# Two attention visits of a product stream merged into one, with PSUM banks shared and sums of 512 columns

## The chip, the cores and the metric

The kernel runs on one core of a Trainium2 chip. The metric is the device time of one execution in microseconds (us), lower being better. Engines are named as in the profile: PE is TensorE (PEld its weight loads), DVE is VectorE, ACT is ScalarE, POOL is GpSimd, SP is SyncE, which issues most DMAs.

## The reference

All data are fp32. x is 8 x 1024 x 1024, the memory is 8 x 64 x 512, W_mem is 1024 x 512, W_gate is 1024 x 2048.

```python
memory_proj = einsum('bme,de->bmd', memory, W_mem)
scores = einsum('bnd,bmd->bnm', x, memory_proj) / sqrt(1024)
attn = softmax(scores)
memory_context = einsum('bnm,bmd->bnd', attn, memory_proj)
gate = sigmoid(einsum('bnf,df->bnd', concat([x, memory_context]), W_gate) + b_gate)
fused = x + gate * memory_context
out = fused * rsqrt(mean(fused**2) + 1e-6) * norm_w
```

## The kernel before

**Setup.** The memory is projected, and the right half of W_gate is applied to it once, so that the gate's second half becomes attention times a 64-row table. Each batch has a tile `mg` of 128 partitions: rows 0 to 63 hold the projection, rows 64 to 127 the projection times the gate weights, with the bias. One set of attention weights `attnT` thus gives both the context (from the upper half) and the gate's addend (from the lower half); `attnT` holds the attention on both halves of its partitions.

**The main loop** takes 16 quads, each of 512 rows of x (four row tiles of 128; two quads are a batch). The gate's product of x with the left half of W_gate is done by two levels of the Winograd form of Strassen's method. The outer level has seven products, in the fixed order of `ORDER`: 1, 6, 7, 5, 4, 2, 3. Each outer product is an inner Winograd product of seven steps, A, B, C, D, A again, E, F; a step is two calls of `mm` (L92), which the profile shows as four matmul passes of 256 columns, since fp32 takes two passes. Steps count slots, 7 to an outer product and 49 to a quad.

**Left operands.** POOL forms four sums `l` for each inner product, one product ahead (`inner_s`): s1 and s2 in the first slots (part 0), s3 and s4 in slot 5 (part 1, slot 2 ahead of product 5). s1 goes into D, s2 into B, s3 into C, s4 into F. DVE forms the outer sums `s` of 1024 columns (`outer_s`), and transposes the next quad's x in eight parts of 512 columns (`transpose_x`, L355): two beside product 5, one in slot 36, two beside product 2, one in slot 38, and two in slots 42 and 43.

**Inner sums.** ACT copies A's sum to p1 (L821). DVE forms u2 = p1 + B, u3 = u2 + C, u4 = u2 + D. POOL adds u3 twice and u4 once, 256 columns at a time, into the output blocks (`pre`, the pre-sums: gate<-gate,u), and DVE adds the sums A, D, E and F from PSUM into the same blocks (`fin`). Product 5 has two blocks to add to, product 1 none to start from. All of an engine's instructions keep the order in which the program issues them.

**A visit** is what the change is about. In each of products 5, 4, 2 and 3, after the second A, PE does eight pairs of passes with the 64-row operands: the context `pc` from the upper half of the rows and the gate's addend from the lower half, which is accumulated onto A, F, E and D. The two halves of the rows run side by side. For its addends product 5 and 2 use attention itself, or the difference of two row tiles' attention (`attn_difference`, one instruction of DVE). After a visit come the sigmoid of the gate block (ACT, L668), `gated` (DVE: gate times pc, gate<-gate,pc), and, later in the next quad, `residual` (a DMA of POOL's queue that adds x), `square` (ACT), and `norm` (DVE, L697: two of 512 columns for each row tile), and the store.

**Order.** `at(slot, fn)` puts a function ahead of the product step of that slot; `step()` runs what is due. `mid((q, o), fn)` puts a function after the visit of product o (`beside`). The scores of the next quad (psT, 16 calls) come after the visit of product 3, their transposes (sc) after product 6's B, the attention's transposes (pa) after product 7's D.

**PSUM.** Five banks b0 to b4 turn over among the products' sums, sc holds the scores and the transposes, and two banks (ctx) hold the two pc.

Of the kernel before, what the change touches and what calls it, by code (L numbers as in the profile page):

```python
# [8 lines left out]
F32 = mybir.dt.float32  # L9
AF = mybir.ActivationFunctionType  # L10
ALU = mybir.AluOpType
# [9 lines left out]
def tile_gated_cross_attention_rmsnorm(  # L21
# [72 lines left out]
    def tt(eng, o, a, b, op):  # L94
        pin(eng.tensor_tensor(o, a, b, op))  # L95
# [4 lines left out]
    def t4k(pool, shape, tag, name):  # L100
        return pool.tile(shape, F32, tag=tag, name=name)
# [9 lines left out]
    banks = [f"b{i}" for i in range(5)]  # L111

    def bank(n, shape, name):
        return ps.tile(shape, F32, tag=banks[n % 5], name=name)

# [3 lines left out]
    pz = bank(0, [P, C], "pz")  # L119
# [89 lines left out]
    pt = [bank(4, [P, BM], "pt0")]  # L209
    pt += [ps_ctx.tile([P, BM], F32, tag="ctx", name=f"pt{k}") for k in (1, 2)]  # L210
    pt += [ps.tile([P, BM], F32, tag="sc", name="pt3")]
# [20 lines left out]
    setup_banks = ["b0", "b1", "b2", "b3", "b4", "ctx", "ctx", "sc"]  # L232
# [169 lines left out]
    def scores(q):  # L402

        pst = ps.tile([P, 2 * P], F32, tag="sc", name=f"psT{q}")
# [10 lines left out]
        sTs[q] = t4k(small, [P, 2, P], "sT", f"sT{q}")  # L415
        pin(nc.scalar.copy(sTs[q].rearrange("p t c -> p (t c)"), pst))

    def transpose_scores(q):
        sc = ps.tile([P, 4, M], F32, tag="sc", name=f"sc{q}")
# [24 lines left out]
    def transpose_attn(q):  # L444
        attn = attns.pop(q)
        pa = ps.tile([P, 2, P], F32, tag="sc", name=f"pa{q}")
# [9 lines left out]
        at = attnTs[q] = t4k(small, [P, 6, P], "attnT", f"attnT{q}")  # L456
# [146 lines left out]
    def at(slot, fn, *args):  # L603
        due.setdefault(slot, []).append(lambda: fn(*args))
# [5 lines left out]
    ORDER = ((1, None), (6, None), (7, None), (5, (1, 1, 2)), (4, (1, 0, 2)), (2, (0, 0, 0)), (3, (0, 1, 4)))  # L610
    SLOTS = 49

    def plan(q):
        t0 = SLOTS * q
        nxt = q + 1 < NQ
        order = [o for o, _ in ORDER]
        for i, o in enumerate(order):
            for part, t in ((0, 1), (1, 2 if o == 7 else 5)):
                if i + 1 < len(order):
                    at(t0 + 7 * i + t, inner_s, q, order[i + 1], part)  # L620
                elif nxt:
                    at(t0 + 7 * i + t, inner_s, q + 1, order[0], part)
# [141 lines left out]
    def outer_product(q, o, ext):  # L764

        nonlocal slot, banks
        l11, l12, l21, l22 = quarters(left(q, o))
        s1, s2, s3, s4 = (L2[q, o][:, i, :, :] for i in range(4))
        kb = {}

        def product(name, tag, lhsT, s, start=True):
            nonlocal slot
            step()
            if name not in kb:
                kb[name] = ps.tile([P, C], F32, tag=banks[tag], name=f"k{name}{q}_{o}")
            for k in range(2):
                mm(kb[name], lhsT[:, k, :], w_op(o, s)[:, k, :], start and k == 0, k == 1)
            slot += 1

        def o_blocks(row, h):  # L780

            for t in (2 * row, 2 * row + 1):
                if (q, t) not in O:
                    O[q, t] = t4k(gpool, [P, D], "gate", f"gate{q}_{t}")
            return [
                O[q, 2 * row + r][:, h * H + n * C : h * H + (n + 1) * C]
                for r in range(2)
                for n in range(2)
            ]


        sums = {
            1: [(o_blocks(0, 0), None)],
            6: [(o_blocks(0, 1), (0, 0))],
            7: [(o_blocks(1, 0), (0, 1))] if o == 7 else [],
            5: [(o_blocks(1, 1), (1, 0)), (o_blocks(0, 1), (0, 1))] if o == 5 else [],
            4: [(o_blocks(1, 0), (1, 0))] if o == 4 else [],
            2: [(o_blocks(0, 0), (0, 0))] if o == 2 else [],
            3: [(o_blocks(0, 1), (0, 1))] if o == 3 else [],
        }[o]  # L800
        sums = [(dst, src and o_blocks(*src)) for dst, src in sums]

        def pre(n, u):

            for dst, src in sums:
                if src is not None:
                    tt(nc.gpsimd, dst[n], src[n], u, ALU.add)

        def fin(n, name, u):
            for dst, src in sums:  # L810
                if src is not None:
                    tt(nc.vector, dst[n], (src if u is None else dst)[n], kb[name], ALU.add)
                elif u is not None:
                    tt(nc.vector, dst[n], u, kb[name], ALU.add)
                else:
                    pin(nc.scalar.copy(dst[n], kb[name]))
# [3 lines left out]
        product("A", 0, l11, R11)  # L820
        pin(nc.scalar.copy(p1, kb["A"]))  # L821
        product("B", 1, s2, T2)
        tt(nc.vector, u2, p1, kb["B"], ALU.add)
        product("C", 2, s3, R12)
        tt(nc.vector, u3, u2, kb["C"], ALU.add)
        pre(3, u3)
        pre(2, u3)
        product("D", 3, s1, T1)
        tt(nc.vector, u4, u2, kb["D"], ALU.add)
        pre(1, u4)  # L830
        product("A", 0, l12, R21, False)
        pcs = []
        if ext:
            row, h, g = ext
            at_, mg = attnTs[q], mgs[q // QPB]
            for n in ("E", "F"):
                kb[n] = ps.tile([P, C], F32, tag=banks[4 if n == "E" else 1], name=f"k{n}{q}_{o}")
            for r, names in ((0, ("A", "F")), (1, ("E", "D"))):
                pc = ps_ctx.tile([P, H], F32, tag="ctx", name=f"pc{q}_{o}_{r}")
                for n in range(2):  # L840
                    cols = slice(h * H + n * C, h * H + (n + 1) * C)
                    mm(
                        pc[:, n * C : (n + 1) * C],
                        at_[0:M, 2 * row + r, :],
                        mg[0:M, cols],
                        n == 0,
                        True,
                    )
                    mm(
                        kb[names[n]],  # L850
                        at_[M:P, g + r, :],
                        mg[M:P, cols],
                        names[n] in "EF",
                        True,
                    )
                pcs.append(pc)
        for fn in beside.pop((q, o), ()):
            fn()
        fin(0, "A", None)
        fin(3, "D", u3)  # L860
        product("E", 4, l22, T4, not ext)
        fin(2, "E", u3)
        if ext:
            sigmoid(q, 2 * row + 1, h)
            last = q + 1 == NQ
            if last:
                at(slot + 2, last_gated, 2 * row + 1, h, pcs[1])
            else:
                at(slot + 1, gated, q, 2 * row + 1, h, pcs[1])
        product("F", 1, s4, R22, not ext)  # L870
        fin(1, "F", u4)
        if ext:
            sigmoid(q, 2 * row, h)
            if last:
                at(slot + 3, last_gated, 2 * row, h, pcs[0])
            else:
                at(slot + 2, gated, q, 2 * row, h, pcs[0])
        if o in (4, 3) and q + 1 == NQ:
            c, d = 2 * ext[0], 2 * ext[0] + 1
# [7 lines left out]
        elif o in (4, 3):  # L887

            row = ext[0]
# [14 lines left out]
        banks = [banks[i] for i in (2, 3, 0, 4, 1)]  # L904
        del L2[q, o]

    for q in range(NQ):
        plan(q)
        for o, ext in ORDER:
            outer_product(q, o, ext)  # L910
# [29 lines left out]
```

## Time and profile before

| what | value |
|---|---|
| median of 3 runs | 971.56 us (971.49 to 972.56) |
| span of the profiled execution | 969.8 us |
| median less that span | 1.8 us |
| PE busy | 957.6 us, 4984 matmul passes |
| DVE busy | 819.9 us, 1484 instructions |
| POOL busy | 763.5 us, 890 instructions |
| ACT busy | 330.4 us, 604 instructions |
| a quad, from psT to the next psT (463.16 and 518.01 us) | 54.85 us |

The page gives the span of the profiled execution, from its first to its last instruction, and no separate time for what lies around it. In a timeline the columns are the start in us, the length in us, the engine, the line, the operation, what is written from what is read, the shapes, and a count where equal instructions were merged; the length of matmuls contains their pipelined end, so the step from start to start is the rate. An idle time ahead of an instruction stands in brackets with what ended it.

### The profile page before, as it was taken

What the parts mean: (1) busy time and instruction counts of PE and PEld (TensorE: products, weight loads), DVE (VectorE), ACT (ScalarE), POOL (GpSimd) and SP (SyncE); (2) the same over time, 40 slices, a digit from 0 to 9 for tenths busy, and PEclk for the clock granted to TensorE, in tenths of its full rate; (3) what the DMA queues carried; (4) which work ended last, traced back from release to release, by engine and by line L of the source; (5) the groups of instructions that cost most, each with busy time, mean ns of one, the idle gap of its engine ahead of it and who ended that gap; (6) DMA issues with size and microseconds to landing.
All of it is one profiled execution on the core that took longest, in us unless ns stands there. A gap on an engine that the chain in (4) does not pass through costs nothing.

```text
span 969.8 us, 14401 instructions
## 1 busy us (share of the span) xinstructions
PE 957.6 (99%) x4984; PEld 772.7 (80%) x4984; DVE 819.9 (85%) x1484; ACT 330.4 (34%) x604; POOL 763.5 (79%) x890
## 2 busy tenths in 40 slices
PE   9999999999999999999999999999999999999995
PEld 8546888788888888788888878788888878888884
DVE  6989879889797988879797978979797978979787
ACT  3000234161423334161433324152433325152345
POOL 4998868778786978878786978878687978878692
PEclk9999999999999999999999999999999999999998
DMA  9857483473919374482918375481917365391712
GB/s 374 273 144 172 88 139 91 118 165 77 173 66 172 111 130 99 111 173 69 182 66 162 101 136 114 102 182 57 193 66 150 112 133 118 88 195 50 189 66 87
DMA packets 70919, 128.32 MB, mean 132 GB/s; under 512 B 12352, under 2 KB 49216, under 8 KB 70592
## 3 DMA queue, kind: packets, MB, share of 16 engines
q1 hardware_dynamic: 61664, 93.86, 37.0%
q0 software_dynamic: 9184, 33.56, 18.8%
q8 instruction: 39, 0.64, 0.3%
q14 instruction: 32, 0.26, 0.1%
HBM read 87.56 MB, written 41.68 MB: 133 GB/s over the span
## 4 chain that ended last, share of the span: by engine, by line
PE 98%; DMA 1%; DVE 0%; ACT 0%; POOL 0%; SPq 0%; issue 0%; DVEq 0%
PE kA L92 20%; PE pc L92 12%; PE kE L92 11%; PE kD L92 10%; PE kF L92 10%; PE kB L92 10%; PE kC L92 10%; PE psT L92 6%; PE pg L92 5%; PE pm L92 2%; DMA wm<-in_w_mem_t 1%; PE pa L449 0%; PE sc L423 0%; DVE gate L755 0%; DVE gate L95 0%; ACT L762 0%
## 5 line engine op out<-in xcount | busy, mean ns | idle before, releaser
L95 POOL TENSOR_TENSOR gate<-gate,u 128x256 f32<-128x256 f32 x336 | 287.8, 888 | 106.9 <-DVE u L95 106.9
L668 ACT ACTIVATE gate<-gate 128x512 f32<-128x512 f32 x128 | 80.6, 631 | 306.3 <-DVE gate L95 305.7
L355 DVE STREAM_TRANSPOSE a<-xq 128x512 f32<-128x512 f32 x128 | 138.2, 1102 | 2.6 <-POOL it L95 2.6
L95 POOL TENSOR_TENSOR l<-a 128x256 f32<-128x256 f32 x128 | 121.7, 951 | 21.7 <-PE kA L92 21.7
L92 PE MATMUL pc<-mg,attnT 64*128 64x256 f32 x512 | 127.5, 389 | 0.0
L92 PE MATMUL kB<-it,l 128*128 128x256 f32 x448 | 115.1, 379 | 0.6 <-DVE gate L95 0.6
L92 PE MATMUL kD<-it,l 128*128 128x256 f32 x448 | 115.0, 379 | 0.0
L92 PEld LDWEIGHTS pc<-mg,attnT 64*128 64x128 f32 x512 | 90.6, 186 | 29.9 <-issue 21.2
L697 DVE SCALAR_TENSOR_TENSOR gate<-gate,ss,nw_sb 128x512 f32<-128x512 f32 x120 | 109.9, 926 | 1.1
L95 POOL TENSOR_TENSOR l<-s 128x256 f32<-128x256 f32 x96 | 79.2, 825 | 34.2 <-PE kF L92 34.1
L92 PE MATMUL kA<-w,a 128*128 128x256 f32 x384 | 98.6, 379 | 0.0
L92 PEld LDWEIGHTS kB<-it,l 128*128 128x128 f32 x448 | 85.0, 190 | 12.5 <-DVE gate L95 1.0
L92 PEld LDWEIGHTS kD<-it,l 128*128 128x128 f32 x448 | 85.1, 190 | 11.6
L95 DVE TENSOR_TENSOR gate<-gate,pc 128x512 f32<-128x512 f32 x128 | 87.0, 680 | 0.4 <-ACT gate L668 0.4
L95 DVE TENSOR_TENSOR gate<-gate,kE 128x256 f32<-128x256 f32 x112 | 45.6, 420 | 47.4 <-PE kE L92 41.4
L92 PEld LDWEIGHTS kA<-w,a 128*128 128x128 f32 x384 | 71.7, 190 | 9.5 <-issue 0.5
L821 ACT COPY u<-kA 128x256 f32<-128x256 f32 x112 | 40.6, 362 | 110.6 <-PE kA L92 106.3
L92 PE MATMUL kE<-it,a 128*128 128x256 f32 x256 | 69.0, 392 | 0.0
L682 ACT ACTIVATE junk<-gate 128x1024 f32<-128x1024 f32 x60 | 63.5, 1058 | 11.2 <-DMA gate<-in_x 10.2
L92 PE MATMUL kA<-t,s 128*128 128x256 f32 x256 | 65.8, 379 | 0.0
L92 PE MATMUL kF<-w,l 128*128 128x256 f32 x256 | 65.7, 379 | 0.0
L92 PE MATMUL kC<-w,l 128*128 128x256 f32 x256 | 65.7, 379 | 0.0
(143 smaller groups left out, 2042.6 us busy)
## 6 DMA issues: line engine op xcount, KB each, us to landing
xq<-in_x SPq DMA_DIRECT2D x64, 512.0 KB, 10.2
gate<-in_x POOLq DMA_DIRECT2D x60, 512.0 KB, 8.3
out<-gate SPq DMA_DIRECT2D x60, 512.0 KB, 2.6
w<-in_w_gate_t SPq DMA_DIRECT2D x8, 512.0 KB, 10.2
w<-in_w_gate_t SPq DMA_DIRECT2D x2, 2048.0 KB, 16.8
mg<-mgd SPq DMA_DIRECT2D x16, 256.0 KB, 3.8
wm<-in_w_mem_t SPq DMA_DIRECT2D x4, 512.0 KB, 6.4
mpd<-mpT SPq DMA_DIRECT2D x4, 512.0 KB, 7.1
```

Source lines behind the costliest of these rows:

```text
L92: pin(nc.tensor.matmul(o, lhsT, rhs, start=start, stop=stop, skip_group_check=True))
L95: pin(eng.tensor_tensor(o, a, b, op))
L355: nc.vector.transpose(A[key][:, :, r * P : (r + 1) * P], chunks(xq[q][:, 4 * t : 4 * t + 4, :], KD)[:, half * KH : (half + 1) * KH],)
L668: pin(nc.scalar.activation(g, g, AF.Sigmoid))
L682: nc.scalar.activation(junk, O[q, t], AF.Square, accum_out=ss[:, t % 2 : t % 2 + 1])
L697: nc.vector.scalar_tensor_tensor(g[:, cols], g[:, cols], rstd[:, t % 2 : t % 2 + 1], nw_sb[:, cols], ALU.mult, ALU.mult,)
L821: pin(nc.scalar.copy(p1, kb["A"]))
```

## The change

- The visits of 5 and 4 are done together, and those of 2 and 3: both after C of the second product (4 or 3), by `visit`. The first product's sums stay in PSUM until then (`held`).
- A product has two banks, `af` for A and F and `ed` for E and D, and there are two such pairs in turn. One bank b takes every B (kB) and one bank c every C (kC); b also takes psT. The visit of the first product puts its two pc into b and c, that of the second into ctx. In product 3 ACT copies the first of these pc to a tile `pe` in SBUF. sc and pa move to ctx.
- The order of steps becomes A, B, C, (visits), E, D, F, A. What was `mid` beside the visit of 5 or 2 comes after that product's C. In the second products D already contains an addend when u4 is taken from it, so F's addend uses a further difference (`NEG`), for which `attn_difference` gets a second instruction.
- The sums in PSUM are added by DVE in 512 columns (`fin_ed`, `fin_af`), POOL's pre-sum with u3 has 512 columns, that with u4 256. For product 1 a copy from PSUM goes from ACT to DVE, in two parts of 256 for row tile 0.
- For the first product of a pair the sums and the sigmoids run after the visits.

```diff
-    ORDER = ((1, None), (6, None), (7, None), (5, (1, 1, 2)), (4, (1, 0, 2)), (2, (0, 0, 0)), (3, (0, 1, 4)))
+    ORDER = (1, 6, 7, 5, 4, 2, 3)
...
+        tt(nc.vector, at[M:P, 6:8, :], at[M:P, 2:6:2, :], at[M:P, 3:6:2, :], ALU.subtract)
...
+    EXT = {5: (1, 1, 2), 4: (1, 0, 2), 2: (0, 0, 0), 3: (0, 1, 4)}
+    SECOND = {4: 5, 3: 2}
+    NEG = {4: 6, 3: 7}
...
+    def visit(q, o, pcs, af, ed):
+
+        row, h, g = EXT[o]
+        at_, mg = attnTs[q], mgs[q // QPB]
+        second = o in SECOND
+        for r, k in ((0, af), (1, ed)):
+            for n in range(2):
+                cols = slice(h * H + n * C, h * H + (n + 1) * C)
+                mm(
+                    pcs[r][:, n * C : (n + 1) * C],
+                    at_[0:M, 2 * row + r, :],
+                    mg[0:M, cols],
+                    n == 0,
+                    True,
+                )
+                left = NEG[o] if second and r == 0 and n == 1 else g + r
+                mm(k[:, n], at_[M:P, left, :], mg[M:P, cols], second and r == 1 and n == 0, True)
+
+    def pre(q, o, u3, u4):
+
+        for dst, src in SUMS[o]:
+            if src is None:
+                continue
+            if u3 is not None:
+                d, a = blocks(q, dst[0], 1, dst[1]), blocks(q, src[0], 1, src[1])
+                tt(nc.gpsimd, d, a, u3.unsqueeze(1).to_broadcast([P, 2, C]), ALU.add)
+            if u4 is not None:
+                d, a = blocks(q, dst[0], 0, dst[1]), blocks(q, src[0], 0, src[1])
+                tt(nc.gpsimd, d[:, 1], a[:, 1], u4, ALU.add)
...
+        step()
+        kc = bank("c", [P, C], f"kC{q}_{o}")
+        product(kc, s3, R12, True)
+        tt(nc.vector, u3, u2, kc, ALU.add)
+        pre(q, o, u3, None)
+        if second:
+            f = SECOND[o]
+            faf, fed, fu3, fu4 = held.pop((q, f))
+            frow, fh, _ = EXT[f]
+            fp = [bank(t, [P, H], f"pc{q}_{f}_{r}") for r, t in enumerate("bc")]
+            visit(q, f, fp, faf, fed)
+            if o == 3 and nxt:
+                pe = t4k(small, [P, H], "pe", f"pe{q}")
+                pin(nc.scalar.copy(pe, fp[0]))
+                fp[0] = pe
+            pcs = [ps_ctx.tile([P, H], F32, tag="ctx", name=f"pc{q}_{o}_{r}") for r in range(2)]
+            visit(q, o, pcs, af, ed)
+        if second:
+            one = slice(0, 1)
+            fin_af(q, f, faf, fu4, one)
+            gate(q, 2 * frow, fh, fp[0], 0)
+            fin_ed(q, f, fed, fu3, one)
+            gate(q, 2 * frow + 1, fh, fp[1], 1)
+            rest = slice(1, 2)
+            fin_af(q, f, faf, fu4, rest)
+            fin_ed(q, f, fed, fu3, rest)
         for fn in beside.pop((q, o), ()):
             fn()
...
+        step()
+        product(ed[:, 0], l22, T4, not second)
+        step()
+        product(ed[:, 1], s1, T1, False)
+        tt(nc.vector, u4, u2, ed[:, 1], ALU.add)
+        pre(q, o, None, u4)
+        first = o in SECOND.values()
+        if first:
+            held[q, o] = af, ed, u3, u4
+        else:
+            fin_ed(q, o, ed, u3)
+        if second:
+            row, h, _ = EXT[o]
+            gate(q, 2 * row + 1, h, pcs[1], 1)
+        step()
+        product(af[:, 1], s4, R22, False)
+        step()
+        product(af[:, 0], l12, R21, False)
+        if not first:
+            fin_af(q, o, af, u4)
+        if second:
+            gate(q, 2 * row, h, pcs[0], 1)
```

`gate` issues the sigmoid and puts `gated` w slots later. `fin_ed` and `fin_af` add a bank of two blocks into the output blocks in one instruction of 512 columns (row tile 0 of product 1, and of 7, takes two of 256).

More of the change, by code (lines that the diff above doesn't have):

```diff
@@ L109, in chunks, with bank @@
         return t.rearrange("p s e -> p (s e)").rearrange("p (m j) -> p j m", j=n)
-    banks = [f"b{i}" for i in range(5)]
-    def bank(n, shape, name):
-        return ps.tile(shape, F32, tag=banks[n % 5], name=name)
+    def bank(tag, shape, name):
+        return ps.tile(shape, F32, tag=tag, name=name)
     zeros = t4k(small, [P, C], "junk", "zeros")
     pin(nc.vector.memset(zeros, 0.0))
-    pz = bank(0, [P, C], "pz")
+    pz = bank("af0", [P, C], "pz")
     for _ in range(4):
@@ L207, in transpose_mem @@
             )
-    pt = [bank(4, [P, BM], "pt0")]
+    pt = [bank("b", [P, BM], "pt0")]
     pt += [ps_ctx.tile([P, BM], F32, tag="ctx", name=f"pt{k}") for k in (1, 2)]
-    pt += [ps.tile([P, BM], F32, tag="sc", name="pt3")]
+    pt += [bank("c", [P, BM], "pt3")]
     def outer_sum(o, a, b, k=slice(0, 4)):
@@ L231, in tile_gated_cross_attention_rmsnorm @@
     (m11, m12), (m21, m22) = mpT
-    setup_banks = ["b0", "b1", "b2", "b3", "b4", "ctx", "ctx", "sc"]
+    setup_banks = ["af0", "ed0", "af1", "ed1", "b", "ctx", "ctx", "c"]
     setup_next = 0
@@ L402, in scores @@
     def scores(q):
-        pst = ps.tile([P, 2 * P], F32, tag="sc", name=f"psT{q}")
+        pst = bank("b", [P, 2 * P], f"psT{q}")
         mpb = mps[q // QPB]
@@ L414, in scores @@
                 )
-        sTs[q] = t4k(small, [P, 2, P], "sT", f"sT{q}")
+        sTs[q] = t4k(small, [P, 2, P], "e", f"sT{q}")
         pin(nc.scalar.copy(sTs[q].rearrange("p t c -> p (t c)"), pst))
     def transpose_scores(q):
-        sc = ps.tile([P, 4, M], F32, tag="sc", name=f"sc{q}")
+        sc = ps_ctx.tile([P, 4, M], F32, tag="ctx", name=f"sc{q}")
         sT = sTs.pop(q)
@@ L445, in transpose_attn @@
         attn = attns.pop(q)
-        pa = ps.tile([P, 2, P], F32, tag="sc", name=f"pa{q}")
+        pa = ps_ctx.tile([P, 2, P], F32, tag="ctx", name=f"pa{q}")
         for t in range(2):
@@ L454, in transpose_attn @@
             )
-        at = attnTs[q] = t4k(small, [P, 6, P], "attnT", f"attnT{q}")
+        at = attnTs[q] = t4k(small, [P, 8, P], "attnT", f"attnT{q}")
         for g in (1, 0):
@@ L615, in plan @@
         nxt = q + 1 < NQ
-        order = [o for o, _ in ORDER]
-        for i, o in enumerate(order):
+        for i, o in enumerate(ORDER):
             for part, t in ((0, 1), (1, 2 if o == 7 else 5)):
-                if i + 1 < len(order):
-                    at(t0 + 7 * i + t, inner_s, q, order[i + 1], part)
+                if i + 1 < len(ORDER):
+                    at(t0 + 7 * i + t, inner_s, q, ORDER[i + 1], part)
                 elif nxt:
-                    at(t0 + 7 * i + t, inner_s, q + 1, order[0], part)
+                    at(t0 + 7 * i + t, inner_s, q + 1, ORDER[0], part)
         if q == 0:
@@ L762, in sqrt_table, with blocks @@
         pin(nc.scalar.activation(t, eps_sb, AF.Sqrt))
-    def outer_product(q, o, ext):
-        nonlocal slot, banks
+    def blocks(q, row, r, h):
+        t = 2 * row + r
+        if (q, t) not in O:
+            O[q, t] = t4k(gpool, [P, D], "gate", f"gate{q}_{t}")
+        return O[q, t].rearrange("p (n c) -> p n c", c=C)[:, 2 * h : 2 * h + 2]
+    SUMS = {
+        1: [((0, 0), None)],
+        6: [((0, 1), (0, 0))],
+        7: [((1, 0), (0, 1))],
+        5: [((1, 1), (1, 0)), ((0, 1), (0, 1))],
+        4: [((1, 0), (1, 0))],
+        2: [((0, 0), (0, 0))],
+        3: [((0, 1), (0, 1))],
+    }
@@ new lines, in tile_gated_cross_attention_rmsnorm @@
+    EXT = {5: (1, 1, 2), 4: (1, 0, 2), 2: (0, 0, 0), 3: (0, 1, 4)}
+    SECOND = {4: 5, 3: 2}
+    NEG = {4: 6, 3: 7}
+    sets = 0
+    held = {}
+    def visit(q, o, pcs, af, ed):
[14 more added lines that the diff above has]
+                mm(k[:, n], at_[M:P, left, :], mg[M:P, cols], second and r == 1 and n == 0, True)
@@ new lines, in pre, with fin_ed @@
+    def pre(q, o, u3, u4):
[8 more added lines that the diff above has]
+                tt(nc.gpsimd, d[:, 1], a[:, 1], u4, ALU.add)
+    def fin_ed(q, o, ed, u3, n=None):
+        for dst, src in SUMS[o][n] if n is not None else SUMS[o]:
+            d = blocks(q, dst[0], 1, dst[1])
+            tt(nc.vector, d, u3.unsqueeze(1).to_broadcast([P, 2, C]) if src is None else d, ed, ALU.add)
@@ new lines, in fin_af @@
+    def fin_af(q, o, af, u4, n=None):
+        for dst, src in SUMS[o][n] if n is not None else SUMS[o]:
+            d = blocks(q, dst[0], 0, dst[1])
+            if src is None:
+                pin(nc.vector.tensor_copy(d[:, 0], af[:, 0]))
+                tt(nc.vector, d[:, 1], u4, af[:, 1], ALU.add)
+            elif src == dst:
+                tt(nc.vector, d, d, af, ALU.add)
+            elif src[0] == dst[0]:
+                a = O[q, 2 * dst[0]].rearrange("p (n c) -> p n c", c=C)[:, 0:4:3]
+                tt(nc.vector, d, a, af, ALU.add)
+            else:
+                tt(nc.vector, d[:, 0], blocks(q, src[0], 0, src[1])[:, 0], af[:, 0], ALU.add)
+                tt(nc.vector, d[:, 1], d[:, 1], af[:, 1], ALU.add)
@@ L767, in outer_product, with gate, product @@
+    def gate(q, t, h, pc, w):
+        sigmoid(q, t, h)
+        if q + 1 == NQ:
+            at(slot + w, last_gated, t, h, pc)
+        else:
+            at(slot + w, gated, q, t, h, pc)
+    def outer_product(q, o):
+        nonlocal slot, sets
         l11, l12, l21, l22 = quarters(left(q, o))
         s1, s2, s3, s4 = (L2[q, o][:, i, :, :] for i in range(4))
-        kb = {}
-        def product(name, tag, lhsT, s, start=True):
+        nxt = q + 1 < NQ
+        af = bank(f"af{sets}", [P, 2, C], f"af{q}_{o}")
+        ed = bank(f"ed{sets}", [P, 2, C], f"ed{q}_{o}")
+        sets ^= 1
+        second = o in SECOND
+        def product(out, lhsT, s, start):
@@ L772, in product @@
             nonlocal slot
-            step()
-            if name not in kb:
-                kb[name] = ps.tile([P, C], F32, tag=banks[tag], name=f"k{name}{q}_{o}")
             for k in range(2):
-                mm(kb[name], lhsT[:, k, :], w_op(o, s)[:, k, :], start and k == 0, k == 1)
+                mm(out, lhsT[:, k, :], w_op(o, s)[:, k, :], start and k == 0, k == 1)
             slot += 1
[L780 to L789, printed above, removed]
@@ L792, in outer_product @@
[L792 to L801, printed above, removed]
@@ L803, in pre @@
[L803 to L816, printed above, removed]
@@ L818, in outer_product @@
         ut = t4k(rot, [P, 4, C], "u", f"u{q}_{o}")
         p1, u2, u3, u4 = (ut[:, i, :] for i in range(4))
[L820 to L856, printed above, removed]
+        step()
@@ new lines, in outer_product @@
+        product(af[:, 0], l11, R11, True)
+        pin(nc.scalar.copy(p1, af[:, 0]))
+        step()
+        kb = bank("b", [P, C], f"kB{q}_{o}")
+        product(kb, s2, T2, True)
+        tt(nc.vector, u2, p1, kb, ALU.add)
+        step()
[15 more added lines that the diff above has]
+            visit(q, o, pcs, af, ed)
@@ L857, in outer_product @@
+        if second:
[7 more added lines that the diff above has]
+            fin_ed(q, f, fed, fu3, rest)
         for fn in beside.pop((q, o), ()):
             fn()
[L859 to L877, printed above, removed]
@@ L878, in outer_product @@
-        if o in (4, 3) and q + 1 == NQ:
-            c, d = 2 * ext[0], 2 * ext[0] + 1
+        step()
[7 more added lines that the diff above has]
+            held[q, o] = af, ed, u3, u4
+        else:
+            fin_ed(q, o, ed, u3)
+        if second:
+            row, h, _ = EXT[o]
+            gate(q, 2 * row + 1, h, pcs[1], 1)
@@ L880, in outer_product @@
+        step()
+        product(af[:, 1], s4, R22, False)
+        step()
+        product(af[:, 0], l12, R21, False)
[3 more added lines that the diff above has]
+            gate(q, 2 * row, h, pcs[0], 1)
+        if second and not nxt:
+            c, d = 2 * row, 2 * row + 1
             if o == 3:
@@ L886, in outer_product @@
                 at(slot + w_, last_norm, t, h_)
-        elif o in (4, 3):
-            row = ext[0]
+        elif second:
             c, d = 2 * row, 2 * row + 1
@@ L903, in outer_product @@
                     at(slot + w_, norm, q, t, h_)
-        banks = [banks[i] for i in (2, 3, 0, 4, 1)]
         del L2[q, o]
@@ L908, in tile_gated_cross_attention_rmsnorm @@
         plan(q)
-        for o, ext in ORDER:
-            outer_product(q, o, ext)
+        for o in ORDER:
+            outer_product(q, o)
     while due:
```

## The prediction

> **What bounds the kernel now.** I read the page from the top: the busy shares, then the chain that ended last.
>
> ```profile
> PE 957.6 (99%) x4984; PEld 772.7 (80%) x4984; DVE 819.9 (85%) x1484; ACT 330.4 (34%) x604; POOL 763.5 (79%) x890
> ...
> PE 98%; DMA 1%; DVE 0%; ACT 0%; POOL 0%; SPq 0%; issue 0%; DVEq 0%
> ```
>
> TensorE (PE) sets the time, and VectorE (DVE) and GpSimd (POOL) are not far behind. Who waited for whom on PE, next, gives 2.1 us in all, one wait of it in the main loop. So time is gained only by shortening PE's own stream, and lost wherever a changed order makes PE wait. Two quads one after another (463.20 to 572.90 us, table by stretches) give 54.85 us of PE in each, with DVE 46.5 and POOL 43.7 us busy: a quad has 8 to 11 us of room there on average. What counts is the order inside it, so I read each engine's timeline in the quad whose product 1 begins at 468.59 us.
>
> PE around the visit of product 4 (passes left out):
>
> ```profile
> 498.79 1.03 PE L92 MATMUL kA<-t,a 128*128 128x256 f32 x4
> 499.74 0.48 PE L92 MATMUL pc<-mg,attnT 64*128 64x256 f32 x1
> ...
> 500.06 0.38 PE L92 MATMUL pc<-mg,attnT 64*128 64x256 f32 x1
> ...
> 500.28 0.38 PE L92 MATMUL pc<-mg,attnT 64*128 64x256 f32 x1
> ...
> 501.67 1.13 PE L92 MATMUL kE<-it,a 128*128 128x256 f32 x4
> 502.64 0.59 PE L92 MATMUL kF<-t,l 128*128 128x256 f32 x2
> ```
>
> Passes follow each other every 0.216 us, a product of four every 0.863 us. At a change of tiling two steps are longer: 499.74 to 500.06 is 0.32, and kE to kF is 0.97. One change costs about 0.197 us (0.31 + 0.32 - 2 x 0.216), a visit has two, so a visit costs 8 x 0.216 + 0.39 = 2.12 us.
>
> POOL, and the PE product that reads its result s3 (`l`):
>
> ```profile
> 491.96 4.17 POOL L95 TENSOR_TENSOR gate<-gate,u 128x256 f32<-128x256 f32 x6 [1.13 <-DVE u L95]
> 496.10 0.72 POOL L95 TENSOR_TENSOR l<-a 128x256 f32<-128x256 f32 x1
> ```
>
> ```profile
> 497.06 1.03 PE L92 MATMUL kC<-t,l 128*128 128x256 f32 x4
> ```
>
> The s3 of product 4 lands at 496.82, and its product C starts at 497.06: 0.24 us of room, with no wait shown. This is the tightest place in the quad.
>
> DVE, just ahead of that:
>
> ```profile
> 489.73 0.51 DVE L95 TENSOR_TENSOR attnT<-attnT 64x256 f32<-64x256 f32 x1
> 490.27 0.42 DVE L95 TENSOR_TENSOR u<-u,kB 128x256 f32<-128x256 f32 x1
> ...
> 490.80 0.75 DVE L697 SCALAR_TENSOR_TENSOR gate<-gate,ss,nw_sb 128x512 f32<-128x512 f32 x1
> 491.47 0.41 DVE L95 TENSOR_TENSOR u<-u,kC 128x256 f32<-128x256 f32 x1
> ...
> 492.13 2.11 DVE L355 STREAM_TRANSPOSE a<-xq 128x512 f32<-128x512 f32 x2
> ```
>
> C of product 5 ended at 489.75 and DVE can read 0.27 us later (kF's product ends at 503.50, its sum starts at 503.77), yet u3 comes only at 491.47: DVE runs 1.4 us late here, and POOL waits for it.
>
> **What the change takes from PE.** The number of matmuls stays. Four visits become two of double length, and four changes of tiling go: 4 x 0.197 = 0.79 us a quad, 12.6 us over 16. A double visit is not in this trace; between nothing saved and all saved I take all, since the second half only continues the same tiling. The new waits of PE on its own earlier writes (pc's second bank in 4, banks of 2) are for work long done: 0.
>
> **Edits that cost nothing.** 512-column sums replace pairs: DVE 0.60 apiece start to start (pc's row, mean 680) against 2 x 0.33. Product 1's copy moves from ACT to DVE (0.35) where DVE has 3.5 us of work in 6.04. ACT's new 512-column copy `pe` has most of the 2.7 us of visits to run in, ACT being 34% busy; without that cover psT would wait its 0.6 us. One bank for kB and one for kC: between two uses lie five products, 4.3 us, except that the visit of 5 or 2 takes both banks right after C, and so waits for u2 and u3. u3 ends 0.27 + 0.41 after C when DVE is on time, and its bank is needed only after half a visit (1.0 us): hidden.
>
> **First cost: product 4's C waits for POOL.** In 5 the visit goes, so C of 4 is due 2.12 us earlier, at 494.94. What feeds it comes later. POOL's queue now reads: pre-sums of 5 with u3 (two of 512), with u4 (two of 256), then s3. No pre-sum of this shape is in the trace: 512-column POOL rows run from 1.27 us (it from w) to 2.27 (w from w, beside DVE); I take 1.27, since the 256-column ones here also run at their undisturbed step of 0.69. Walk:
> - Product 6's u4 stands behind a norm (478.96, 0.98) and ends at 480.35, so POOL's sum with u4 ends at 481.17, where before it ended at 480.89. Its next six operations took 5.28 us: 486.45. Pre-sum of 7: 487.72.
> - DVE waits for it with the 512 sum: 487.85 to 488.45; s sum 1.32, 489.8; two sums of 7, 490.45; attention differences, now two of 0.54, 491.5; u2 491.85; reciprocal and norm 492.7; u3 493.1. That is 1.2 us later than before.
> - POOL: two of 1.27 to 495.75. u4 now stands behind the two transposes (to 495.1), ends at 495.5 and holds nothing up. Two of 0.69: 497.13. A norm runs beside it; the two norms from 499.64 us (2.25 us) lie beside three POOL sums that took 2.99 us instead of 2.07, so 0.46 more for each norm, which I half count: 497.4. s3: 498.1, and 0.05 to PE.
>
> Wait: 498.15 - 494.94 = 3.2 us. Lower bound: s3 lands when it did before, 496.82, 1.9 us. Upper bound: contention in full and 0.3 on the pre-sums, 3.8. Quad 0 has DVE weight sums and quad 15 no transposes there; POOL is what binds, so all 16 count: 51 us.
>
> **Second cost: product 3's C waits for DVE.** Times from the end of 4's C. Half a visit 1.0, then 0.27. DVE's queue: two sums 1.3 to 1.9 and 2.2 to 2.8 (the second after the whole visit of 5), two more 4.0, two norms 5.4, two products with pc 6.6, u4 7.0, sum 7.6, sigmoid on ACT 0.75 (504.11 less 503.37), pc 8.95, sum 9.55, transpose 10.6, pc 11.2, u2 and u3 of product 2 11.85, three transposes 14.95, u4 15.3. POOL: 0.1 + 0.7 for its pre-sum, 0.7 for s3, 0.05: 16.85. PE: two visits 3.85, four products 3.45, product 2 (its visit gone) 6.04, A and B 1.73: 15.07. Wait 1.8 us; before, s3 of 3 landed at 509.92 for a C at 513.40. Bounds 0.9 (0.1 less at each of nine handovers) and 2.7 (both norms beside POOL). Quad 15 has no transposes left: 15 x 1.8 = 27 us. What was queued behind, u2 of product 3, ends at 17.65, as C ends: no third wait. Product 3 with its psT (13.4 us of PE) and product 1 let DVE and POOL catch up.
>
> **Sum.** The profiled span is 969.8 us, 1.8 below the median of the three runs, 971.56; what lies around it I leave alone, and the tail (10.2 us after the last product) loses or gains under 0.5. 971.5 - 12.6 + 51 + 27 = 1037 us.
>
> **A rule that speaks against it.** The array does start slowly in this trace:
>
> ```profile
> 1.19 3.78 PE L92 MATMUL pz<-zeros 128*128 128x256 f32 x8 [1.19 <-DVE zeros L118]
> ```
>
> Eight passes take 3.78 us, about twice the later step of 0.216, while the granted clock reads 1.00. The Trainium skill, TensorE: Matmul & The Clock Gate, section "What's actually happening", says that the array falls to half rate after an idle window of some 3.4 us and needs as long to recover; no row here shows that in mid-run. An estimate from that page: if every first wait set it off, 1.7 us a quad, 27 us more, 1064 us.
>
> **Rivals.**
> - Faster: DVE and POOL keep up, only the 0.79 us counts: 959 us. It decides below 0.79 us of waits a quad. For it: both engines have 8 us of room a quad. Against: s3 of 4 has 0.24 us of room and its product moves 2.12 us forward; even with u3 on time POOL is free only at 490.83, and 3.9 us of pre-sums and 0.7 of s3 end at 495.4, 0.5 late. 6%.
> - Only one wait appears: C of 4 alone 971.5 - 12.6 + 51 = 1010; C of 3 alone 986. For it: the second hangs on the sum of twenty DVE steps. 22%.
> - The array also slows after the waits, or they are at their upper bounds: 971.5 - 12.6 + 61 + 40 = 1060. 14%.
> - The waits just pay for the saving, within 0.2% (about 2 us, what a measurement of this kernel can tell from no change): 2%.
>
> My case has 56%. The lower bounds with the lower rivals reach 1000 (-12.6 + 30 + 13 = 1002), the upper 1062; that leaves out the faster case and part of C of 3 alone. Slower: 56 + 22 + 14 = 92%.
>
> **What would show it.** Right: PE's waits name POOL l before kC in product 4, 2 to 4 us in each quad, and again in product 3; the quad is near 59 us; double visits last 3.85 us; POOL's 512 sums about 1.3 us. Wrong: a quad near 54.1 us and no PE waits, or waits at the visits' banks (DVE u) instead.

## The result, and the profile after

| | before | changed |
|---|---|---|
| median | 971.5 us (970.98 to 972.56) | 1074.2 us (1071.68 to 1076.25) |
| ratio | 1 | 1.1055 (95% interval 1.1038 to 1.1073) |
| span of the profiled execution, its own time | 969.8 us | 1071.8 us, 1073.56 us |
| a quad, psT to psT | 54.85 us | 61.29 us (502.76 to 564.05) |

The change makes the kernel 10.6% slower; 1037 us was forecast, with a range that ended at 1062. The page of the changed kernel, first the busy times, then the engines of the chain that ended last:

```profile
PE 978.6 (91%) x4984; PEld 791.7 (74%) x4984; DVE 829.0 (77%) x1292; ACT 338.2 (32%) x603; POOL 709.2 (66%) x778
...
PE 49%; DVE 30%; POOL 12%; issue 6%; ACT 2%; DMA 1%; DVEq 0%; SPq 0%; POOLq 0%
```

PE no longer carries the chain: 42% of it runs through DVE and POOL. PE is also *busy* for longer (978.6 us against 957.6) with the same 4984 passes, although four changes of tiling a quad are gone. So there are two losses, waiting and slower work. Who waited on PE, next (total us, times, longest):

```profile
PE kC L92 <- POOL l L95: 79.6, 33, 3.6
```

That is all of the main loop's waiting, and 32 of the 33 waits stand where the forecast put them (the other is at C of product 2 in the last quad). PE's timeline in one quad, with the products' passes around C of 4 and C of 3 (in brackets the wait ahead of the line):

```profile
535.40 1.03 PE L92 MATMUL kB<-it,l 128*128 128x256 f32 x4
539.95 1.50 PE L92 MATMUL kC<-t,l 128*128 128x256 f32 x4 [3.52 <-POOL l L95]
...
546.30 1.13 PE L92 MATMUL ed<-it,a 128*128 128x256 f32 x4
...
556.77 1.03 PE L92 MATMUL kB<-it,l 128*128 128x256 f32 x4
559.34 1.13 PE L92 MATMUL kC<-w,l 128*128 128x256 f32 x4 [1.54 <-POOL l L95]
```

PE idles 3.68 us ahead of C of 4 (from the end of B's four passes at 536.27) and 1.71 us ahead of C of 3. Product 4's C and its double visit then take 6.35 us (539.95 to 546.30); the same work in product 3 takes 4.71 (559.34 to 564.05). Why, the table by stretches shows (the stretch, its length, the busy time of PE, PEld, DVE, ACT and POOL, the granted clock as the third number from the end, DMA share and GB/s):

```profile
536.00:540.00 4.00, 0.47 (x3) 0.07 (x2) 2.28 (x4) 1.31 (x2) 4.00 (x6) 1.00 0.30 121
540.00:542.00 2.00, 2.00 (x8) 1.22 (x10) 0.42 (x1) 0.00 (x0) 1.92 (x3) 0.64 0.05 21
542.00:544.00 2.00, 2.00 (x12) 1.65 (x10) 0.42 (x1) 0.00 (x0) 1.29 (x2) 0.50 0.00 0
544.00:546.00 2.00, 2.00 (x22) 1.74 (x20) 1.55 (x4) 1.18 (x2) 0.00 (x0) 1.00 0.00 0
```

The clock is granted in full while PE idles, and at half just after: 12 passes in 2 us where the next stretch has 22. In the record of the clock these half-rate stretches are 3.413 us long (one, at 967.24 us, is twice that), and they begin at whole multiples of 3.413 us from one another: 113.91, 175.35, 236.79 and 356.25 us, for instance, lie 18, 18 and 35 times 3.413 apart. So the clock is set for one fixed window at a time. One quad out of the sixteen had the same wait and no half-rate stretch:

```profile
292.00:296.40 4.40, 0.93 (x5) 0.47 (x3) 2.78 (x5) 1.66 (x2) 4.40 (x6) 1.00 0.24 98
296.40:298.40 2.00, 1.95 (x12) 1.50 (x14) 0.42 (x1) 0.00 (x0) 1.92 (x3) 1.00 0.13 51
```

There PE idled from 292.76 to 296.45. The border of two windows, counted on from the other stretches, lies at 294.81, so 2.05 and 1.64 us of idle time fell into two windows; in the quad above 2.79 us of it fell into one. The quad with the split gap is 59.67 us long, its neighbours 61.15 and 61.31.

What feeds C of 4, first POOL (the pre-sums of product 5, then s3), then DVE up to u3 of product 5:

```profile
534.90 4.32 POOL L95 TENSOR_TENSOR gate<-gate,u 128x512 f32<-128x512 f32 x4 [2.70 <-DVE u L95]
539.18 0.72 POOL L95 TENSOR_TENSOR l<-a 128x256 f32<-128x256 f32 x1
```

```profile
529.79 1.81 DVE L95 TENSOR_TENSOR s<-a,s 128x1024 f32<-128x1024 f32 x1
...
533.74 0.75 DVE L694 SCALAR_TENSOR_TENSOR gate<-gate,ss,nw_sb 128x512 f32<-128x512 f32 x1
534.40 0.41 DVE L95 TENSOR_TENSOR u<-u,kC 128x256 f32<-128x256 f32 x1
```

POOL idles 2.70 us for u3, then spends 4.32 us on pre-sums before it comes to the sum that PE is waiting for. DVE is late with u3, because sums, the attention differences and a norm stand ahead of it.

Ahead of C of 3 it is DVE, which has three transposes between u3 and u4 of product 2; POOL's pre-sum with u4, and s3 behind it, wait for them:

```profile
554.40 3.08 DVE L352 STREAM_TRANSPOSE a<-xq 128x512 f32<-128x512 f32 x3
557.40 0.39 DVE L95 TENSOR_TENSOR u<-u,ed 128x256 f32<-128x256 f32 x1
```

### The profile page after: what moved, and what is told of

Its sections match the earlier page's. It is cut to its first block, busy times and chain, and to the rows that moved or that the text cites. A ratio compares the mean times of both kernels' runs of the same rounds, so it can differ in the third digit from the quotient of the medians.

```text
span 1071.8 us, 14142 instructions
## 1 busy us (share of the span) xinstructions
PE 978.6 (91%) x4984; PEld 791.7 (74%) x4984; DVE 829.0 (77%) x1292; ACT 338.2 (32%) x603; POOL 709.2 (66%) x778
## 3 DMA queue, kind: packets, MB, share of 16 engines
q0 software_dynamic: 9184, 33.56, 16.7%
## 4 chain that ended last, share of the span: by engine, by line
PE 49%; DVE 30%; POOL 12%; issue 6%; ACT 2%; DMA 1%; DVEq 0%; SPq 0%; POOLq 0%
PE pc L92 10%; PE af L92 10%; POOL gate L95 9%; DVE gate L95 9%; PE ed L92 7%; DVE gate L694 6%; PE kC L92 6%; DVE u L95 6%; PE psT L92 5%; PE pg L92 4%; DVE a L352 4%; PE kB L92 3%; POOL l L95 2%; PE pm L92 2%; DVE s L95 2%
## 5 line engine op out<-in xcount | busy, mean ns | idle before, releaser
L95 POOL TENSOR_TENSOR gate<-gate,u 128x512 f32<-128x512 f32 (+1 forms) x224 | 242.8, 1097 | 306.1 <-DVE u L95 297.1
L92 PE MATMUL ed<-it,l 128*128 128x256 f32 x448 | 115.0, 379 | 0.0
L863 ACT COPY u<-af 128x256 f32<-128x256 f32 x112 | 41.1, 367 | 225.6 <-PE af L92 225.4
L92 PE MATMUL kC<-t,l 128*128 128x256 f32 x192 | 55.3, 414 | 55.6 <-POOL l L95 55.6
L95 DVE TENSOR_TENSOR gate<-gate,af 128x512 f32<-128x512 f32 (+1 forms) x128 | 77.3, 614 | 36.7 <-PE af L92 36.7
L95 DVE TENSOR_TENSOR gate<-gate,ed 128x512 f32<-128x512 f32 x112 | 76.5, 683 | 34.8 <-POOL gate L95 23.6
L92 PE MATMUL af<-w,a 128*128 128x256 f32 x384 | 98.5, 379 | 0.0
L95 DVE TENSOR_TENSOR u<-u,kC 128x256 f32<-128x256 f32 x112 | 47.0, 419 | 64.0 <-PE kC L92 58.6
L92 PEld LDWEIGHTS ed<-it,l 128*128 128x128 f32 x448 | 83.9, 190 | 10.7
L92 PE MATMUL af<-mg,attnT 64*128 64x256 f32 x256 | 82.5, 450 | 0.0
```

Of the source, the lines that this page charges most:

```text
L92: pin(nc.tensor.matmul(o, lhsT, rhs, start=start, stop=stop, skip_group_check=True))
L863: pin(nc.scalar.copy(p1, af[:, 0]))
```

## The experiments

All are edits of the changed kernel, each timed beside the kernel before on the same chip; ratios are to that kernel.

### POOL's s3 ahead of the pre-sums

The s3 and s4 of product 4 are formed ahead of product 5's pre-sums.

```diff
-            for part, t in ((0, 1), (1, 2 if o == 7 else 5)):
+            for part, t in ((0, 1), (1, 2 if o in (7, 5) else 5)):
```

> POOL forms s3 and s4 of product 4 ahead of the pre-sums of product 5. Theory of the queue order: C of 4 no longer waits (3.7 us a quad now), the half-rate window goes with it (1.6 us), but the visit of 5 then waits for u2 of 4, which stands on DVE behind two transposes and a norm, about 1.2 us; C of 3 still waits 1.6. 1074 - 16 x 5.4 + 16 x 1.2 = 1007 us. Rival, POOL has too much to do in products 5 and 4 whatever the order: the wait turns up at another operand of POOL's with about its old length, 1060 to 1075 us.

1019.4 us, ratio 1.0492 (1.0462 to 1.0523): 55 us less than the changed kernel. The wait at C of 4 is gone, and with it all but three of the half-rate stretches of the main loop. So one edit of POOL's order removes both, and the first cost is POOL's queue, as forecast. The wait came back in part at the next place, the bank that the visit needs:

```profile
518.47 0.48 PE L92 MATMUL pc<-mg,attnT 64*128 64x256 f32 x1 [1.90 <-DVE u L95]
```

1.2 us was expected here, and the 16 waits sum to 25.8 us, 1.6 each and 2.0 at most: 6.6 of the 12 us by which the expectation was too low. The three half-rate stretches, at about 1.6 us each, are most of the rest. DVE's lateness with u2 and u3, which the forecast had called hidden behind half a visit, is not hidden once POOL is out of the way.

### Extra products in the gap: the clock by itself

Ahead of C of 4, PE does product B once more (then, in a second kernel, three times more) into C's bank, which C writes afresh. The extra work touches neither DVE nor POOL; it only fills idle time.

```diff
         kc = bank("c", [P, C], f"kC{q}_{o}")
+        if o == 4:
+            for k in range(2):              # second kernel: (0, 1) * 3
+                mm(kc, s2[:, k, :], w_op(o, T2)[:, k, :], k == 0, k == 1)
```

> Product B of 4 is computed a second time into the bank of C, ahead of C: 0.86 us of PE work more, inside the wait, and nothing else is moved. Theory of the clock window: PE is now idle for 2.8 us instead of 3.7, no half-rate window follows, and the time falls by 16 x 1.6 to 1048 us with the waits' end unchanged. Rival, the slow passes after the wait belong to the visit (its operands, or its banks) and not to the idle time: 1074 us, same slow passes.

1073.4 us, ratio 1.1048 (1.1016 to 1.1080): nothing gained. The gap fell to 2.7 to 2.9 us (3.2 in the first quad), less than one window of 3.413 us, and the half rate stayed in 14 of the 16 quads:

```profile
480.15 1.29 PE L92 MATMUL kC<-t,l 128*128 128x256 f32 x4 [2.67 <-POOL l L95]
```

```profile
482.00:484.00 2.00, 2.00 (x12) 1.66 (x10) 0.43 (x1) 0.00 (x0) 1.49 (x2) 0.50 0.00 0
```

So a gap need not fill a window. Sorting the windows of this run and of the changed kernel that ran at the full rate by PE's idle time within them: those with 1.76 us or less were followed by the full rate, those with 2.13 us or more by the half rate, in between (1.89 to 2.05) it went either way. A window that itself runs at the half rate needs less: the one at 967.24 us in the changed kernel had 1.61 us of idle time, and the next was at the half rate too. The new theory: about 2 us in one window decide. It says that three extra products, which leave a gap of 1 us, must remove the half rate.

> Product B of 4 is computed three times more into the bank of C instead of once: PE is idle some 1.1 us before C of 4, where it was 2.8 with one filler and 3.7 with none. Theory of the fixed windows, as the records of the changed kernel and of the run with one filler suggest it (a window of 3.41 us with more than about 2 us of idle time makes the next window half rate): no half-rate window can follow, C of 4 still starts when POOL is ready, and the time falls by 16 x 1.6 us to 1047 us, although PE does 41 us more work than in the changed kernel. Rival, the slow passes belong to the visit after a POOL wait of any length: 1073 us as with one filler.

1049.3 us, ratio 1.0799 (1.0777 to 1.0820), as expected. PE does 2.6 us more work in each quad, C of 4 begins when it did, and the kernel is 25 us faster than the changed one:

```profile
530.85 1.13 PE L92 MATMUL kC<-t,l 128*128 128x256 f32 x4 [0.90 <-POOL l L95]
```

C's four passes take their usual 1.13 us instead of 1.50, and no half-rate stretch is left in the main loop. This is the price of the clock alone: 25 us, or 1.6 us a quad, apart from the wait that sets it off.

### Two transposes earlier: the second wait

The transposes of slots 36 and 38, ahead of u4 of product 2 on DVE, go to slots 17 and 18.

```diff
-        for i, t, half in ((36, 0, 0), (38, 1, 0), (42, 0, 1), (43, 1, 1)):
+        for i, t, half in ((17, 0, 0), (18, 1, 0), (42, 0, 1), (43, 1, 1)):
```

> The two transposes of slots 36 and 38 (around product 2) move to slots 17 and 18 (product 7). Theory for the second wait: DVE reaches u4 of product 2 some 2 us earlier, C of 3 no longer waits (1.7 us a quad less); in exchange DVE is 0.5 us later at product 5 and C of 4 waits 4.2 us. 1074 - 15 x 1.8 + 16 x 0.5 = 1055 us. Rival, POOL's own length sets the second wait: it stays, 1080 us.

1076.9 us, ratio 1.1084 (1.1051 to 1.1116). The wait at C of 3 falls from 1.54 to 0.35 us, so DVE's transposes made it; but the transposes now delay u3 of product 5:

```profile
482.23 2.08 PE L92 MATMUL kC<-t,l 128*128 128x256 f32 x4 [3.81 <-POOL l L95]
...
501.45 1.13 PE L92 MATMUL kC<-w,l 128*128 128x256 f32 x4 [0.35 <-POOL l L95]
```

From the ninth quad to the last but one the wait at C of 3 is 0.2 us at most, also in the ninth itself, where one window alone ran at the half rate, as in the changed kernel. The time went from one place to the other: the first wait grew to 3.8 us in most quads and 5.0 at most, with the half rate behind it for two windows (6.83 us) in 14 of the 16 quads. The expectation of 1055 had left that second effect out.

### Four visits again

The visits of 5 and 2 go back to the end of their own products (with all pc in ctx); the banks, the order of steps and the sums of 512 columns stay.

```diff
         if not first:
             fin_af(q, o, af, u4)
+        if first:
+            frow, fh, _ = EXT[o]
+            fp = [ps_ctx.tile([P, H], F32, tag="ctx", name=f"pc{q}_{o}_{r}") for r in range(2)]
+            visit(q, o, fp, af, ed)
...
```

> Four visits again, the visits of 5 and 2 at the end of their own products, all pc in the ctx banks; order of steps, banks and sums of 512 columns as in the changed kernel. Theory: the visit of 5 gives POOL its 2.12 us back, C of 4 waits 1.5 to 1.7 us and without a half-rate window, C of 3 no longer; some 0.7 us at a pc bank in product 3. 971.5 + 16 x 1.7 + 16 x 0.7 = 1010 us (995 to 1015). Rival, the order of steps (D after E) and the longer sums delay POOL, and the place of the visits is innocent: 1060 us or more.

1033.8 us, ratio 1.0640 (1.0609 to 1.0671); 1010 was expected. The wait at C of 4 and the half rate are gone (but for one stretch near the end), so merging is what brought C of 4 forward. Yet the quad takes 58.53 us: the rest of the change costs 62 us without any merging. In DVE's timeline u4 of product 5 stands behind two transposes, and the visit, in the new order of steps, follows at once upon D, from which u4 must first be read:

```profile
517.35 2.10 DVE L352 STREAM_TRANSPOSE a<-xq 128x512 f32<-128x512 f32 x2
519.36 0.38 DVE L95 TENSOR_TENSOR u<-u,ed 128x256 f32<-128x256 f32 x1
```

```profile
519.80 0.48 PE L92 MATMUL ed<-mg,attnT 64*128 64x256 f32 x1 [0.98 <-DVE u L95]
```

To see whether this order is the cost, the two transposes went behind u4 (slot 26):

```diff
-            mid((q, 5), transpose_x, q + 1, t, 0)
+            at(t0 + 26, transpose_x, q + 1, t, 0)
```

> Four visits as in the earlier run with the visits apart, with the two transposes beside product 5 put behind u4 of 5 on DVE. That run waited 1.1 us a quad for u4 of 5 at the visit's ed bank, and about 1.5 us at pc banks. Theory, the new order of steps (D after E, so u4 behind the transposes) is a cause beside the merging: the wait at ed goes, the other waits stay, 1034 - 16 x 1.1 = 1016 us. Rival, DVE's load as such: the two transposes then delay the sums and gates after the visit, the waits at pc grow by as much, 1030 us or more.

1034.6 us, ratio 1.0647 (1.0626 to 1.0669): the rival held. The wait on u4 goes; C of 4 (13.8 us in all) and the visits' banks (23.4 us against 16.7) take its place. In both orders DVE is late by about as much, so its work in the three products ahead counts more than the order there; the next step is to move work out of them.

### Moving DVE's work out of the products ahead of the visits

POOL's s3 and s4 of products 4 and 3 go ahead of the pre-sums of 5 and of 2; transposes are spread (one stays beside 5; `early` issues one right behind the first double visit and two behind the second, two go to slots 32 and 33); the first two row tiles are normalised 18 to 22 slots later, except in the last two quads.

```diff
-            for part, t in ((0, 1), (1, 2 if o == 7 else 5)):
+            for part, t in ((0, 1), (1, 2 if o in (7, 5, 2) else 5)):
...
-        for i, t, half in ((36, 0, 0), (38, 1, 0), (42, 0, 1), (43, 1, 1)):
+        for i, t, half in ((32, 0, 0), (33, 1, 0)):
             at(t0 + i, transpose_x, q + 1, t, half)
+        for o, t, half in ((4, 3, 0), (3, 0, 1), (3, 1, 1)):
+            early.setdefault((q, o), []).append(
+                lambda t=t, half=half: transpose_x(q + 1, t, half)
+            )
...
-                when = (17, 18, 23, 29, None, None)
+                late = q + 2 < NQ
+                when = (17, 18, 45, 47, 49, 49) if late else (17, 18, 23, 29, None, None)
```

> The changed kernel with its queues laid out for the merged visits: POOL forms s3 and s4 of 4 and of 3 ahead of the pre-sums; DVE's transposes are spread (one ahead of u4 of 5, one after u3 of 4 during the visits, two into the waits for u4 and for the sigmoid of 4, two after C of 2, two during the visits of 2 and 3), and the four norms of row 0 go to the end of product 3 and the start of 1. Theory, both waits are orders in the queues of POOL and DVE and not their total work: PE waits under 0.5 us a quad, no half-rate windows, 971.5 - 12.6 = 959 us, 957 to 968. Rival, DVE and POOL have too much to do between products 5 and 3 for visits that are merged: a wait of over 0.8 us a quad stays somewhere and the time is not under 971 us.

1033.0 us, ratio 1.0648 (1.0612 to 1.0685), far from the 957 to 968 expected. (This run is called e6_dve_spread below.) Both waits of the changed kernel are gone, and a new one has come, at product 4's first step. PE's wait, and DVE's that lies behind it:

```profile
PE af L92 <- DVE gate L95: 33.2, 13, 3.7
```

```profile
DVE gate L95 <- DMA out<-gate: 63.8, 13, 6.0
```

Product 7's sums need an output buffer whose last content is still being stored. There are seven buffers for four row tiles a quad, and two of them are now held longer. The 13 gaps were 1.8 to 3.8 us, most of them over 2, so the half rate came back behind 11 of them. In SP's queue the load of the next x stood behind the late stores and began 11 to 12.4 us after psT in thirteen quads; in the changed kernel it begins 4.2 us ahead of psT and 1.3 to 1.5 us after it, in turn. So it ran beside the store that DVE waited for: in the quad whose psT is at 480.05 us that store was issued at 500.35, behind this load and one more, and landed 12.9 us later, where 2.6 us is the median in the changed kernel. The next kernel moves that load ahead of the stores:

```diff
-        at(t0 + 2, load_xq, q + 1)
+        if q == 0:
+            at(t0 + 2, load_xq, q + 1)
+        if q + 2 < NQ:
+            at(t0 + 46, load_xq, q + 2)
```

> e6_dve_spread with one more move: the load of the next x tile is issued right after the last of its readers, in slot 46, ahead of the late stores of the first two row tiles on SP's queue, not in slot 2 behind them. In e6_dve_spread this load was issued 11 us after psT (491.0, psT at 480.05), behind stores that waited for the norms, where the changed kernel issues it 1.4 us after psT, so it shared the DMA engines with the next row tiles' store, whose buffer product 7 needs. Theory: that store's delay alone makes the waits at product 4's A. Then they go, no gap of 2 us is left, every window of the clock's record is at the full rate, and the time is 971.5 - 12.6 = 959 us, 957 to 968 as PE's small waits (9 us in e6_dve_spread) stay or go. Rival: seven output buffers are too few once two row tiles are held 22 slots longer, whatever the order of transfers; then 33 us of waits and part of the half-rate windows stay, above 1010 us.

976.3 us, ratio 1.0040 (1.0026 to 1.0055): 57 us less by one moved load (e8_load_ahead below). The seven buffers are not the limit; the load's place in the queue was the cause. Whether the store was late more by what it shared with the load or by its turn in SP's queue is not shown. The forecast of 959 still missed, by 17 us. The waits of PE and of DVE that are left:

```profile
PE kC L92 <- POOL l L95: 7.2, 9, 2.3
```

```profile
DVE gate L831 <- DMA out<-gate: 18.7, 10, 3.5
```

The same store is still late by up to 3.5 us, and most quads are 0.3 to 1.1 us longer than the 54.05 us of the shortest, one 4.2 (with half the clock). In the last quad ACT's squares, waiting for a transfer, hold up PE by 2.3 us.

```diff
-                when = (17, 18, 45, 47, 49, 49) if late else (17, 18, 23, 29, None, None)
+                when = (24, 25, 40, 41, 47, 49) if late else (24, 25, 27, 29, 36, 37)
```

> e8_load_ahead with three times moved, to clear what its trace still shows: DVE's copy of product 1 waits up to 3.5 us for the store of row tile 0 (10 times, 18.7 us), PE then 0.7 to 2.4 us at C of product 7, and in the last quad ACT's squares, which wait 5.6 us for the residual's transfer, hold up the copy p1 of product 5 by 2.3 us. The norms of row tile 0 go to slots 40 and 41, where DVE sits idle 1.4 and 0.4 us in product 2, so that its store leaves some 5 us earlier; the squares of the row go behind product 5's D (slots 24, 25), in the last quad with the norms at 27, 29, 36 and 37. Theory: what is left over the clean quad (54.05 us) is only these waits. The fifteen quads from the first psT to the last then take 802 us instead of 814.3, the stretch behind the last psT about 58 instead of 63.3, and the time is 976 - 12 - 5 = 959 us, 957 to 965, faster than the kernel before by 0.7 to 1.5%. Rival: the merged visits leave so little room that a wait removed comes back elsewhere; then 968 to 978, no faster than before.

973.9 us, ratio 1.0029 (1.0018 to 1.0040); this is e9_norms_in_gaps. All waits for stores are gone, but the rival held: two norms in a row are longer than DVE's idle time, and the visit of product 3 waits for u2 in fourteen quads (some 54.83 us each):

```profile
PE pc L92 <- DVE u L95: 12.8, 17, 1.6
```

So the second norm goes behind that visit:

```diff
-                when = (24, 25, 40, 41, 47, 49) if late else (24, 25, 27, 29, 36, 37)
+                when = (24, 25, 40, 45, 47, 49) if late else (24, 25, 28, 33, 34, 36)
```

> e9_norms_in_gaps with one norm moved in each quad, and the norms of the last quad. There all waits of PE but one are gone: product 3's visit waits 0.85 us in each of fourteen quads for u2 to free its bank, because two norms of 2.4 us together stand ahead of u2, where DVE had 1.4 us of idle time. The second norm goes behind that visit (slot 45), where DVE sits idle 2.0 us; in the last quad the norms go to slots 28, 33, 34 and 36, since two of them (3.13 us beside POOL's sums) hold up product 4's visit by 1.58 us. Theory: nothing else is left, so the quad is the clean one of 54.0 to 54.1 us, no wait of PE in the main loop, and the time is 973.9 - 14 x 0.8 - 1.6 = 961 us, 958 to 964, faster than the kernel before by 1.1%. Rival: the wait comes back elsewhere, as in each version before this one (store of the output, product 7's C); then 968 us or more.

963.1 us (962.74 to 963.55), ratio 0.9907 (0.9890 to 0.9923): 0.9% faster than the kernel before. Its busy times, chain, and waits of PE:

```profile
PE 944.9 (98%) x4984; PEld 776.2 (81%) x4984; DVE 836.9 (87%) x1292; ACT 336.6 (35%) x603; POOL 723.3 (75%) x778
...
PE 93%; DVE 4%; issue 1%; POOL 1%; DMA 1%; ACT 1%; SPq 0%; DVEq 0%; POOLq 0%; ACTq 0%
```

```profile
PE pc L92 <- DVE u L95: 1.7, 2, 0.9
...
PE af L92 <- ACT u L870: 1.1, 1, 1.1
```

PE carries the chain again, with one bank wait in the first quad, and one more and a wait for ACT in the last. Fourteen quads take 54.05 to 54.08 us each. Before, a quad had 54.85, also without a wait and with the same passes. The difference, 0.77 us, is what the merged visits save: in PE's steps of a quad the longer ones at four changes of tiling are gone.

## Why the prediction was wrong, point by point

- **The saving was right.** 0.79 us a quad was forecast from four changes of tiling; the kernel without waits shows 0.77. The double visit does run on in one tiling, as was assumed.
- **C of 4, and why: right, slightly too small.** 3.2 us of wait was forecast, 3.3 to 3.7 us of idle time measured, 58 us over 16 quads against 51. DVE's u3 came 24.9 us after product 1's first step, 0.4 later than walked (the sum s took 1.81 us beside POOL, not 1.32), and that is most of the miss of 0.5: the four pre-sums took 4.3 us, as walked.
- **C of 3: right.** 1.8 us forecast, 1.7 measured; 26 us against 27. The walk was made for the full rate, and there, in the run with three extra products, it held: C of 3 was due 15.1 us after the end of 4's C and s3 came after 16.8, walked 15.1 and 16.9. In the changed kernel the half rate slowed the double visit, and DVE's sums that wait for it, so that both came 1.3 us later (16.4 and 18.1); that the wait kept its length is in part luck. Moving two transposes away took 1.2 us off it.
- **The failed step is the clock.** In the sum it stood at zero, and as a rival at 14%. It cost 1.64 us in 15 of 16 quads (6.35 less 4.71), 25 us, shown by itself by the three extra products. The Trainium skill, TensorE: Matmul & The Clock Gate, section "What's actually happening", told of the half rate and nearly its price (1.7 us was estimated from it), but by its idle window of some 3.4 us the 3.2 us forecast for the wait lay just under the mark. The runs show the mark near 2 us within one window: in the changed kernel none of the first waits left a whole window idle, 3.27 us of one at most. There the measurement decides, and every first wait of 2 us or more was at risk. The trace before also held more than the prediction read from it. Its record of the clock begins only at 5.15 us, so the 1.00 beside the slow first passes was no measurement; and at its end, behind PE's last pass at 959.39 us, it shows 0.50 from 964.30 us on. So the fall to the half rate was on record, but not how little idle time it takes.
- **"Edits that cost nothing": hidden, not free.** The bank waits called hidden do not show in the changed kernel, since POOL's wait covers them; with POOL's order mended they cost 1.6 us a quad (25.8 us).
- **The sum with measured terms:** 971.5 - 12.6 + 58 + 26 + 25 = 1068 us; the tail behind the last pass grew by 1.9 us (12.3 against 10.4) and PE's restart after each of 32 waits adds 0.1, so 1073, against 1073.56 for the profiled execution.
- **The rival "faster"** had its place right (it decides at 0.79 us of waits) and described what the last experiment reached, but only with five kinds of other work moved (POOL's sums, transposes, norms, squares, a load); the change as made is not that case.

What stays open: how much of the 62 us of the unmerged variant each of its parts (shared banks, the order of steps, the sums of 512 columns) costs by itself. PE's idle time explains 2.8 us a quad of the 3.7 us lost; part of the rest are passes that no longer run side by side where one half of a visit waited (two of ed run alone at 520.34 us).

## What to carry to other kernels

Where the bound engine has no waits, merging its work saves what the trace prices, but it also brings the following steps forward: walk each other engine's queue to the new due time, and expect to move their work too, one wait at a time, transfers included. In these runs a wait of TensorE cost more than its length once some 2 us of it fell into one window: look at the granted clock in the stretch behind it. And an edit that a nearer wait hides has a price that appears when that wait is mended.

## What the runs showed of the hardware

- The clock is granted for fixed windows of 3.413 us, at the full or the half rate. PE idle for about 2 us within one window set the next window to half: over the main loops of all the runs a full-rate window with 1.84 us or less never did, one with 2.12 us or more always, and between them it went either way. The same 3.7 us gap, split 2.05 and 1.64 by a window's border, did not. Behind a window that itself ran at the half rate, 0.57 us or less gave the full rate again and 0.76 us or more the half rate once more; so the gaps of 3.8 to 5.0 us of the run with two transposes moved were followed by two half-rate windows.
- Filling such a gap with work of no use made the kernel 25 us faster.
- A load of 2 MB, issued about 1 us ahead of psT instead of 11 to 12.4 us behind it on SP's queue, made 57 us of difference (1033.0 to 976.3 us): DVE's waits for stores fell from 63.8 to 18.7 us, and the half-rate stretches of the main loop from 11 to 2.
